# First layer of a two-layer kernel: the first image's front and first projection cut into chunks beside the first steps, and VectorE's work at an image's end one piece later

## The chip, the cores and the metric

The kernel runs on one core of one Trainium2 chip. The metric is the device time of one execution in microseconds; less is better. Before the change the median of five runs is 6506.6 us (6499.82 to 6520.29).

A core has five engines with queues of their own: TensorE (PE, with its weight loads PEld), VectorE (DVE), ScalarE (ACT), GpSimd (POOL) and SyncE (SP, which here only issues transfers). Each engine works through its queue in order; a result that another engine needs is waited for at the head of the queue, with everything behind it.

## What is computed

Two layers over four images of 48 x 48 positions and 128 channels. The first layer, cut to what matters here:

```
xn = groupnorm(x); xin, z = split(xn @ in_proj.T)            # 128 -> 2 x 256
xc = silu(depthwise_conv3x3(xin) + conv_b)                    # 256 channels, 2304 positions
for k in 0..3:          # by rows, by columns, and both backwards
    dts, Bs, Cs = split(x_proj[k] @ xc_k)                     # 8 + 16 + 16 rows
    dt = softplus(dt_proj[k] @ dts + dt_b[k])                 # 256 x 2304
    for n in 0..15:     # states
        h = scan over positions: h = h * exp(dt * A[k, :, n]) + dt * xc_k * Bs[n]
        ys_k += h * Cs[n]
y = sum of the four ys_k (turned back) + D * xc
x = x + out_proj @ (layernorm(y) * silu(z))
```

The second layer (a spectral attention block over 128 x 128 images) isn't touched by the change.

## The kernel before

Channels lie on the 128 partitions, the 256 inner channels as two halves `f`. The 2304 positions are cut into five chunks (`CHUNKS`, line 34): four of 480 and one of 384. An image has four directions in the order 0, 2, 1, 3 (`ORDER`), so there are 16 directions, 80 chunks and, with 16 states each, 1280 *steps*. The main loop (line 508 on) calls `advance` once a step.

**A step** is spread over ten calls of `advance` by `LAGS` (line 470). In one call each engine gets its share of different steps: SP fetches the broadcast rows of B and C (`fetch`), PE spreads a row of B over the partitions into PSUM, tile `pb` (`spread`, lag 3; a single buffer), DVE multiplies it with `du` = dt x xc into `db` (`drive_in`, lag 4; each fourth step POOL does it, from a transferred row), ACT takes the two exponentials `da` (`decay`, lag 4), DVE runs the scan `h` (`scan`, lag 5), POOL multiplies by C into `hc` (`read_out`, lag 5), PE adds the two halves of `hc` into `yp` (`sum_up`, lag 8), and ACT stores `yp` when a chunk is done (`put_away`, lag 9).

**The side work** is written as generators in a list `later`, and `piece()` (line 454) runs one of them up to its next `yield`; `advance` ends with one piece. A generator that has begun keeps its turn until it yields `FREE` or `WAIT`; else the first of the list that needn't wait is taken. The side work is:

- `front(b)` (line 151): load x of image b, its statistics (`bn_stats`), the scaled weights `w`, and for each half f: nine diagonal matrices of the taps `cdiag` and a cleared padded image `pad` on POOL, the input projection `pj` on PE with ACT writing it into `pad`, then nine matmuls per chunk (`pc`) with ACT writing `xc`; a piece holds one input projection or three taps. Silu over all of `xc` comes last.
- `project` (line 217): for each chunk of the next direction px, a transfer of B and C to DRAM (`cd`), two corrections `less`, and the two halves of dt (`pd`); then Softplus over all five chunks. The ring of seven buffers lets it run at most six chunks ahead (`WAIT`).
- `back` (line 271): for each chunk of an image's last direction the layer norm over channels, the gate and the output projection: PE's mean `pm`, DVE subtracts, ACT squares, PE `pv`, ACT's square root, PE's gate `pz` twice, DVE's reciprocal, Silu, POOL multiplies, PE `po`, DVE multiplies, PE `pr`, DVE adds, store.

All matmuls of the side work use one PSUM bank, `pp` (`side`, line 132), so one's result must be taken away before the next one begins.

`Ordered` (line 36) keeps the instructions of PE, DVE, ACT and POOL in the order in which the program calls them, so what stands in front of what on an engine is decided by these calls. The order of SP's transfers is chosen by the framework.

**The order of things.** Line 502: the first image's `front` is run to its end alone, then the first direction's `project` to its end (lines 504, 505), then `drive` computes `du` for the first chunk on POOL, and only then the steps begin. The other images' fronts run beside steps: at the third chunk (m == 2) of an image's first direction the open `back`s are drained and `front(b + 1)` joins `later`. `drive` for the next chunk is called at steps 8 and 12 of a chunk.

Of the kernel before, what the change touches and what calls it, by code (L numbers as in the profile page):

```python
# [10 lines left out]
F32 = mybir.dt.float32  # L11
# [10 lines left out]
L = T * H  # L22
# [31 lines left out]
def layer0(ctx, tc, io, x1_dram):  # L54
# [20 lines left out]


# [14 lines left out]
    on.gpsimd.memset(w_xp, 0.0)  # L91
    for k in range(K):
        src = io["x_proj_wT"][k].rearrange("(f p) c -> p f c", p=128)
        for o, c0, c1 in ((0, R, R + 2 * N), (32, 0, R), (64, R, R + N), (96, R, R + N)):
            nc.sync.dma_start(w_xp[:, k, :, o : o + c1 - c0], src[:, :, c0:c1])
# [35 lines left out]

    def side(name):
        return ps_s.tile([128, 512], F32, tag="pp", name=name)
# [11 lines left out]
    def load_x(b, name):  # L145
        x = one.tile([128, 1, L], F32, tag="x", name=f"{name}{b}")
        for q in range(4):
            nc.sync.dma_start(x[:, 0, q * 576 : (q + 1) * 576], io["xT"][:, b, q * 576 : (q + 1) * 576])
        return x

    def front(b, made):


        x = load_x(b, "x")
        xc = two.tile([128, NF, L], F32, tag="xc", name=f"xc{b}")
        made["xc"] = xc
        yield FREE
# [20 lines left out]
        yield FREE  # L178
        for f in range(NF):
            cdiag = one.tile([128, 9, 128], F32, tag="cdiag", name=f"cdiag{b}_{f}")  # L180
            for j in range(9):
                on.gpsimd.tensor_scalar(cdiag[:, j], ident, cw[:, f, j : j + 1], None, ALU.mult)
            pad = one.tile([128, T + 2, H + 2], F32, tag="pad", name=f"pad{b}_{f}")
            on.gpsimd.memset(pad, 0.0)
            yield FREE
            for s, n in CHUNKS:
                r0, nr = s // H, n // H
                pj = side(f"pj{b}_{f}_{s}")
                on.tensor.matmul(pj[:, 0:n], w[:, f * 128 : (f + 1) * 128], x[:, 0, s : s + n], start=True, stop=True)
                yield  # L190
                on.scalar.activation(
                    pad[:, 1 + r0 : 1 + r0 + nr, 1 : 1 + H],
                    pj[:, 0:n].rearrange("p (r c) -> p r c", c=H),
                    AF.Identity,
                    bias=wb[:, f : f + 1],
                )
            for s, n in CHUNKS:
                r0, nr = s // H, n // H
                pc = side(f"pc{b}_{f}_{s}")
                for j in range(9):  # L200
                    dy, dx = divmod(j, 3)
                    on.tensor.matmul(
                        pc[:, 0:n].rearrange("p (r c) -> p r c", c=H),
                        cdiag[:, j],
                        pad[:, r0 + dy : r0 + dy + nr, dx : dx + H],
                        start=(j == 0),
                        stop=(j == 8),
                    )
                    if j % 3 == 2:
                        yield  # L210
                on.scalar.activation(xc[:, f, s : s + n], pc[:, 0:n], AF.Identity, bias=cb[:, f : f + 1])
            yield FREE
# [3 lines left out]

    def project(b, k, chunks, xc):

        w_dt = two.tile([32 + R, D], F32, tag="w_dt", name=f"w_dt{b}_{k}")
        nc.sync.dma_start(w_dt[32 : 32 + R], io["dt_proj_wT"][k])
        for c in chunks:
            s, n = c.s, c.n
            while done[0] + RING - 1 < c.number:
                yield WAIT
            src = at(xc, k, s, n)
            px = side(f"px{c.t}")
            for f in range(NF):
                on.tensor.matmul(  # L230
                    like(px[0:NX, 0:n], k), w_xp[:, k, f], src[:, f], start=(f == 0), stop=(f == NF - 1)
                )
            yield
            xd = two.tile([32 + R, LC], F32, tag="xd", name=f"xd{c.t}")
            on.scalar.copy(xd[:, 0:n], px[0 : 32 + R, 0:n])
            c.cd = dram.tile([2 * N, LC], F32, tag="cd", name=f"cd{c.t}")
            nc.sync.dma_start(c.cd[:, 0:n], xd[0 : 2 * N, 0:n])

            c.bs = ring.tile([NX, LC], BF16, tag="bs", name=f"bs{c.t}")
            on.scalar.copy(c.bs[:, 0:n], px[0:NX, 0:n])  # L240
            for q in range(2):
                on.tensor.matmul(px[0:NX, 0:n], less[:, q], c.bs[:, 0:n], start=False, stop=True, skip_group_check=True)
                yield
                rows = slice(64 + 32 * q, NX)
                on.scalar.copy(c.bs[rows, 0:n], px[rows, 0:n])
            c.dt = ring.tile([128, NF, LC], F32, tag="dt", name=f"dt{c.t}")
            for f in range(NF):
                pd = side(f"pd{c.t}_{f}")
                on.tensor.matmul(
                    pd[:, 0:n],  # L250
                    w_dt[32 : 32 + R, f * 128 : (f + 1) * 128],
                    xd[32 : 32 + R, 0:n],
                    start=True,
                    stop=True,
                )
                yield
# [249 lines left out]
    for f in range(NF):  # L506
        drive(directions[0][0], f)
# [655 lines left out]
```

## Time and profile before

| what | value |
|---|---|
| median of five runs | 6506.6 us |
| the profiled execution: its time, its span | 6507.24 us, 6505.4 us |
| mean granted clock of TensorE | 0.833 |
| busy in the span: PE, DVE, ACT, POOL | 4834.9, 5268.8, 3052.8, 4727.3 us |
| first scan starts | 224.1 us |
| last scan starts | 4390.4 us |
| last op of the first layer on DVE starts | 4421.11 us |

The steps of the first layer fill 224 to 4390 us; the second layer runs from 4421 us to the end. In the timeline of VectorE the starts of the scans were counted, 80 to a direction. The time from the first scan of a direction to that of the next is, in us:

| image | direction 0 | 2 | 1 | 3 |
|---|---|---|---|---|
| 0 | 276.0 | 256.4 | 240.5 | 276.4 |
| 1 | 281.0 | 257.1 | 240.5 | 280.2 |
| 2 | 280.7 | 256.8 | 244.5 | 278.9 |
| 3 | 246.5 | 240.3 | 240.4 | 270.2 |

Within a direction eight steps that nothing disturbs take 24.1 us with 480 positions and 19.7 with 384. Images 0 to 2 have the next image's front beside directions 0 and 2; image 3 has none.

In the lines that follow, a window's line gives its bounds, its length, then the busy time of PE, PEld, DVE, ACT and POOL with the number of instructions, TensorE's granted clock, the DMA engines' busy share and GB/s. A timeline's line gives start and duration in us, the engine, the program's line (50 for all that go through `Ordered`), the operation, output<-inputs, the shapes and the count; a bracket holds the idle time before it and what ended it. A tile's view lists how long its engine sat idle before the instructions on it, until what, and how many times.

### The profile page before, as it was taken

How to read it: one execution, taken by the hardware profiler on the slowest of the kernel's cores; microseconds unless marked ns; L12 is line 12 of the kernel's file. 1: busy time of each engine (PE TensorE's matmuls, PEld its weight loads, DVE VectorE, ACT ScalarE, POOL GpSimd, SP SyncE). 2: the span in 40 equal slices, each digit the busy share in tenths (PEclk: the TensorE clock that was granted, in tenths of full speed). 3: DMA queues.
4: the chain of work that ended last, by engine and by line, in shares of the span. 5: the costliest groups of instructions: out<-in, count | busy, mean ns of one | idle time of the engine just before them, and what ended most of it. 6: DMA issues, size and time to landing. Idle time of an engine off the chain costs nothing. (4 is left out here: it accounts for less than half of the span.)

```text
span 6505.4 us, 45606 instructions
## 1 busy us (share of the span) xinstructions
PE 4834.9 (74%) x12650; PEld 2229.8 (34%) x12650; DVE 5268.8 (81%) x3784; ACT 3052.8 (47%) x6633; POOL 4727.3 (73%) x2641
## 2 busy tenths in 40 slices
PE   6788778889787888877888777784233498878663
PEld 2244333334333334333333333332122244435332
DVE  0678999887999897899989999983799899963444
ACT  1556666656666665666666656552000133312222
POOL 1588998887998888899888999981665499941222
PEclk9799999999999999999999999997566655556876
DMA  1222322222233232232323322322100100010222
GB/s 26 68 86 90 100 96 96 91 95 85 98 105 96 89 100 87 89 100 95 96 89 104 101 99 99 96 80 58 44 0 1 16 8 4 4 40 8 59 59 58
DMA packets 271777, 457.65 MB, mean 70 GB/s; under 512 B 87134, under 2 KB 196734, under 8 KB 271522
## 3 DMA queue, kind: packets, MB, share of 16 engines
q1 hardware_dynamic: 224546, 438.13, 21.6%
q10 hardware_dynamic: 46976, 16.61, 1.4%
q8 instruction: 99, 1.62, 0.1%
q14 instruction: 156, 1.28, 0.1%
HBM read 419.60 MB, written 35.02 MB: 70 GB/s over the span
## 5 line engine op out<-in xcount | busy, mean ns | idle before, releaser
L50 POOL TENSOR_TENSOR hc<-h,cbc 128x960 f32<-128x960 f32 (+1 forms) x1280 | 2718.1, 2136 | 521.8 <-DVE h L50 363.1
L50 DVE TENSOR_TENSOR_SCAN h<-da,carry,db 128x961 f32<-128x961 f32 (+1 forms) x1280 | 2698.9, 2129 | 94.1 <-ACT carry L50 62.3
L50 PE MATMUL yp<-hc,ident 128*128 128x480 f32 (+1 forms) x5120 | 2292.1, 578 | 0.5 <-POOL hc L50 0.5
L50 ACT ACTIVATE da<-dt,a_neg 128x480 f32<-128x480 f32 (+1 forms) x2560 | 1666.3, 651 | 1300.1 <-DVE h L50 1254.2
L50 PEld LDWEIGHTS yp<-hc,ident 128*128 128x128 f32 x5120 | 1014.7, 200 | 1539.5 <-issue 970.8
L50 DVE TENSOR_TENSOR db<-du,pb 128x960 f32<-128x960 f32 (+1 forms) x960 | 1063.3, 1108 | 411.1 <-PE pb L50 357.2
L50 PE MATMUL pb<-bs,pick 112*128 112x480 bf16 (+1 forms) x960 | 362.8, 378 | 539.9 <-DVE db L50 538.4
L50 POOL TENSOR_TENSOR db<-du,bbc 128x960 f32<-128x960 f32 (+1 forms) x320 | 687.2, 2147 | 0.0
L928 PE MATMUL py<-attn_t,xt 48*128 48x384 f32 x768 | 507.6, 845 | 78.6 <-DVE m L936 71.6
L930 ACT COPY ysb<-py 128x384 f32<-128x384 f32 x384 | 184.3, 480 | 404.0 <-PE py L928 360.8
L928 PEld LDWEIGHTS py<-attn_t,xt 48*128 48x128 f32 x768 | 233.8, 320 | 339.2 <-issue 147.8
L50 PE MATMUL pc<-pad,cdiag 128*128 128x480 f32 (+1 forms) x720 | 301.5, 559 | 7.6 <-ACT xc L50 6.0
L50 POOL TENSOR_TENSOR du<-dt,xc 128x480 f32<-128x480 f32 (+1 forms) x160 | 204.3, 1277 | 120.8 <-ACT dt L50 120.8
L50 ACT COPY db<-carry 128x1 f32<-128x1 f32 x1280 | 228.6, 179 | 35.5 <-DVE db L50 33.0
L50 PE MATMUL px<-xc,w_xp 128*112 128x480 f32 (+1 forms) x320 | 212.1, 793 | 8.8 <-ACT xc L50 4.9
L848 PE MATMUL pat<-ident,s 48*48 48x48 f32 x128 | 13.3, 277 | 275.6 <-POOL s L844 275.6
L50 PE MATMUL yp<-y,ident 128*128 128x480 f32 (+1 forms) x240 | 175.6, 865 | 40.3 <-ACT y L50 40.3
L941 POOL TENSOR_TENSOR zi<-zi,m 128x384 f32<-128x384 f32 x192 | 191.9, 999 | 14.5
L50 PEld LDWEIGHTS <-pick 112*128 112x128 bf16 x960 | 99.3, 103 | 300.1 <-issue 284.6
L939 POOL TENSOR_TENSOR zi<-gw,ysb 128x384 f32<-128x384 f32 x192 | 181.6, 946 | 25.8 <-ACT ysb L930 25.5
L50 PE MATMUL pd<-xd,w_dt 8*128 8x480 f32 (+1 forms) x320 | 176.4, 632 | 25.4 <-ACT bs L50 14.6
L50 ACT COPY carry<-h 128x2 f32<-128x2 f32 x1024 | 194.4, 190 | 0.0
(263 smaller groups left out, 5626.8 us busy)
## 6 DMA issues: line engine op xcount, KB each, us to landing
cbc<-cd SPq DMA_DIRECT2D x512, 480.0 KB
bbc<-cd SPq DMA_DIRECT2D x256, 240.0 KB
cbc<-cd SPq DMA_DIRECT2D x128, 384.0 KB
bbc<-cd SPq DMA_DIRECT2D x64, 192.0 KB
da_wM<-a_wM SPq DMA_DIRECT2D x12, 396.0 KB
x<-in_xT SPq DMA_DIRECT2D x16, 288.0 KB
xr<-in_xT SPq DMA_DIRECT2D x16, 288.0 KB
e_wM<-de_wM SPq DMA_DIRECT2D x12, 384.0 KB
```

The costliest lines, as they stand in the source:

```text
L50: return lambda *args, **kw: self._tc.keep_in_program_order(emit(*args, **kw))
L848: nc.tensor.transpose(pt[:, h], s[:, h], ident[0:T, 0:T])
L928: nc.tensor.matmul(p[:, 0 : HG * T], xt[:, c, j], attn_t[:, b, hs], start=True, stop=True)
L930: nc.scalar.copy(ysb[:, c], py[c])
L939: nc.gpsimd.tensor_mul(zi[:, hs], gr, ysb[:, 1])
L941: nc.gpsimd.tensor_add(zi[:, hs], zi[:, hs], t2)
```

## The change

- The loads of x for the first image come first; `x_proj` is loaded with four transfers into `w_x` and put into place in `w_xp` by four DVE copies, instead of sixteen transfers.
- `front` is split into `open_up` (statistics and scaled weights), `taps`, `project_in` and `convolve`, and `project` gets its inner part as `project_chunk`; for images 1 to 3 they do what they did.
- The first image has a generator of its own, `boot`: both halves' taps and cleared images are made at the very start (the second half's lie in the buffer of the second `xc`), then for each chunk in turn both halves are projected (with one more row of 48 positions as the convolution's halo), convolved, put through Silu, projected for the first direction, and put through Softplus; a chunk is then `ready`.
- The steps begin when the first chunk is ready. During the first direction each step is followed by a second piece, and `boot` stands first in `later`.
- Until the steps begin, `side` goes round four PSUM banks; then it uses `pp` alone as before.
- `drive` is called at steps 11 and 14 of a chunk instead of 8 and 12; in the first direction it first runs pieces until that chunk is ready.
- In `back` there is one more `yield` ahead of each of three DVE operations: the subtraction after pm, the multiplication after po, the addition after pr.

```diff
+    x_first = load_x(0, "x")
...
+    w_x = const.tile([128, K, NF, R + 2 * N], F32, name="w_x")
     for k in range(K):
...
-            nc.sync.dma_start(w_xp[:, k, :, o : o + c1 - c0], src[:, :, c0:c1])
+        nc.sync.dma_start(w_x[:, k], io["x_proj_wT"][k].rearrange("(f p) c -> p f c", p=128))
+    for o, c0, c1 in ((0, R, R + 2 * N), (32, 0, R), (64, R, R + N), (96, R, R + N)):
+        on.vector.tensor_copy(w_xp[:, :, :, o : o + c1 - c0], w_x[:, :, :, c0:c1])
...
+    banks = deque([(ps_s, "pp"), (ps_b, "pb"), (ps_y, "yp0"), (ps_y, "yp1")])
+    begun = [False]
+
     def side(name):
-        return ps_s.tile([128, 512], F32, tag="pp", name=name)
+        pool, tag = banks[0]
+        if not begun[0]:
+            banks.rotate(-1)
+        return pool.tile([128, 512], F32, tag=tag, name=name)
...
+    def boot(chunks, made):
+        pads = [one.tile([128, T + 2, H + 2], F32, tag="pad", name="pad0")]
+        cdiags = [one.tile([128, 9, 128], F32, tag="cdiag", name="cdiag0")]
+        spare = two.tile([128, NF * L], F32, tag="xc", name="spare")
...
+        for f in range(NF):
+            taps(cdiags[f], f)
+            on.gpsimd.memset(pads[f], 0.0)
+        x = x_first
+        yield from open_up(0, x, made)
+        w_dt = load_dt(0, 0)
+        for c in chunks:
+            s0, s1 = (c.s + H if c.s else 0), min(c.s + c.n + H, L)
+            for f in range(NF):
+                for s in range(s0, s1, LC):
+                    yield from project_in(0, f, x, made, pads[f], s, min(LC, s1 - s))
+                yield from convolve(0, f, cdiags[f], pads[f], made["xc"], c.s, c.n)
+            v = made["xc"][:, :, c.s : c.s + c.n]
+            on.scalar.activation(v, v, AF.Silu)
+            yield from project_chunk(c, w_dt, made["xc"])
+            on.scalar.activation(c.dt[:, :, 0 : c.n], c.dt[:, :, 0 : c.n], AF.Softplus)
+            c.ready = True
+            yield FREE
...
@@ back
             on.tensor.matmul(pm[:, 0:n], lnmat, yb[:, f, 0:n], start=(f == 0), stop=(f == NF - 1))
+        yield
         yield
         on.vector.tensor_sub(ys, ys, pm[:, None, 0:n].to_broadcast([128, NF, n]))
...
         yield
+        yield
         on.vector.tensor_mul(xo[:, 0:n], po[:, 0:n], rs[:, 0:n])
...
         yield
+        yield
         on.vector.tensor_add(xo[:, 0:n], xo[:, 0:n], pr[:, 0:n])
...
-    later.append(front(0, images[0]))
-    drain(later[0])
-    nxt = upcoming(0)
-    drain(nxt)
+    first = directions[0]
+    later.append(boot(first, images[0]))
+    while not first[0].ready:
+        piece()
+    begin()
     for f in range(NF):
-        drive(directions[0][0], f)
+        drive(first[0], f)
...
-                if i in (N // 2, N // 2 + 4):
-                    f = int(i > N // 2)
+                if i in (N // 2 + 3, N // 2 + 6):
+                    f = int(i > N // 2 + 3)
                     if m + 1 < len(chunks):
+                        while not (j or chunks[m + 1].ready):
+                            piece()
                         drive(chunks[m + 1], f)
...
                 advance(Step(c, i))
+                if not j:
+                    piece()
```

## The prediction

> **What bounds the kernel now.** I read the span first, then VectorE's timeline with its 1280 scans counted in eights, then the windows, then the single waits.
>
> ```profile
> 0.00:50.00 50.00, 16.74 (x28) 7.24 (x29) 7.07 (x29) 6.55 (x10) 10.37 (x19) 1.00 0.22 42
> 50.00:100.00 50.00, 39.02 (x92) 16.98 (x90) 0.00 (x0) 4.56 (x7) 7.37 (x10) 0.92 0.00 0
> 100.00:150.00 50.00, 43.09 (x95) 18.84 (x94) 0.00 (x0) 6.13 (x9) 0.00 (x0) 0.88 0.07 24
> 150.00:200.00 50.00, 31.90 (x39) 9.20 (x40) 0.00 (x0) 17.54 (x26) 0.00 (x0) 0.57 0.14 45
> 250.00:300.00 50.00, 38.64 (x92) 16.85 (x92) 49.17 (x30) 30.01 (x76) 47.78 (x24) 0.93 0.31 101
> 400.00:450.00 50.00, 49.27 (x133) 23.73 (x132) 38.68 (x24) 24.27 (x61) 36.73 (x18) 1.00 0.22 70
> 500.00:531.00 31.00, 31.00 (x91) 16.32 (x90) 19.55 (x15) 13.99 (x37) 19.91 (x13) 1.00 0.22 63
> ```
>
> Columns: window, length, busy us of PE, PEld, DVE, ACT, POOL, granted clock, DMA share, GB/s. For 200 us DVE does nothing: the first image's front and first projection run alone. At 250 DVE is full (49 of 50); at 400 to 531 PE is full, because the next image's front is woven in one piece per step.
>
> ```profile
> 220.82 1.16 DVE L50 TENSOR_TENSOR db<-du,pb 128x960 f32<-128x960 f32 x1 [195.01 <-PE pb L50]
> 224.14 2.21 DVE L50 TENSOR_TENSOR_SCAN h<-da,carry,db 128x961 f32<-128x961 f32 x1
> ...
> 483.95 0.96 DVE L50 TENSOR_TENSOR db<-du,pb 128x768 f32<-128x768 f32 x1 [1.19 <-PE pb L50]
> ...
> 259.64 0.56 PE L50 MATMUL pb<-bs,pick 112*128 112x480 bf16 x1 [3.27 <-DVE db L50]
> 259.99 3.03 PE L50 MATMUL yp<-hc,ident 128*128 128x480 f32 x4
> 263.02 0.36 PE L50 MATMUL pb<-bs,pick 112*128 112x480 bf16 x1
> ...
> 481.17 2.58 PE L50 MATMUL pc<-pad,cdiag 128*128 128x480 f32 x6
> 483.58 0.33 PE L50 MATMUL pb<-bs,pick 112*128 112x384 bf16 x1
> ```
>
> The first scan is at 224.1. By the count, eight undisturbed steps take 24.1 us (3.01 a step; 2.47 in a chunk of 384). The first direction's 80 scans take 276.0 instead of 232, the second's 256.4 (its first eight 31.0). Where PE is full a step is the sum of its matmuls: one pass of 480 columns is 0.402 us (481.17 to 483.58 is six), so an fp32 matmul is 0.80, a step's own work (two yp, 3/4 of a pb) 1.76, three taps 2.41.
>
> ```profile
>   PE pm L50: 22.8, 11
>   PE po L50: 45.4, 17
>   PE pr L50: 40.9, 20
> ...
> 4398.68 1.16 DVE L50 TENSOR_TENSOR yb<-yb,pm 128x960 f32<-128x960 f32 x1 [6.16 <-PE pm L50]
> 4403.58 3.15 DVE L50 RECIPROCAL ws<-ws 128x480 f32<-128x480 f32 x1 [3.75 <-ACT ws L50]
> 4416.90 0.66 DVE L50 TENSOR_TENSOR ws<-po,ws 128x480 f32<-128x480 f32 x1 [10.16 <-PE po L50]
> 4421.11 0.66 DVE L50 TENSOR_TENSOR ws<-ws,pr 128x480 f32<-128x480 f32 x1 [3.56 <-PE pr L50]
> ```
>
> The tile views: in 20 `back`s DVE waits 109.1 us, 19.9 of it in the bare tail (the 6.16 is mostly the last read-out; 10.16 and 3.56 are `back`'s own). The tail's last `back`, with nothing beside it, takes 4398.68 to 4421.77 = 23.1 us, of which DVE works 5.6.
>
> **Part 1, the start.** Loads: SP now issues x first, and four w_x loads instead of sixteen (10.86 us). 4x0.475 + 0.40 + 0.42 + 0.43 + 4x0.68 + 0.47 puts w_out's issue at 7.1; it lands 1.9 later as now; four new DVE copies (about 1 us, an estimate from the 0.28 of a 128x128) and the old constants put bn_stats at 12.1 to 15.4 instead of 20.98: 5.6 earlier. The taps and clearings of both halves, 2x(5.24+2.18) on POOL, end near 19.5, before `w` is due, so they cost nothing; if ident landed 2 us later they would cost that much. First projection matmul: 28.05 - 5.6 = 22.4.
>
> Chunk 0: input projection, halo and padding 3.1; first half's taps 10.0 (cold rate, as at 45.76); second half 2.0 + 7.8; ACT copy, Silu table and Silu 2.9; projection chain 12.4 as at 165.38, less 0.75 because four banks rotate; Softplus and table 2.2. Together 39.8: ready at 62.2, against 214.6 now.
>
> What then comes ahead of step 0 on PE's in-order queue decides. In the order in which the changed kernel is built, pb of step 0 stands behind chunk 1's first half (18 passes), two input projections and three taps: 0.9 + 10 + 3.2 + 2.7 = 17 us, so pb at 79, first scan near 86: 138 us earlier than 224.1.
>
> Two pieces a step then follow. A boot chunk is 14 pieces, 7 steps. PE's work: 2 input projections 1.6, 18 taps 14.5, px, less and pd 3.6, 7 steps 12.3 = 32.0. Walking its chain, PE waits 1.2 twice for ACT to pad, 2 for xc, Silu and its table, 1.3 + 0.8 for copies of px, and 3.8 while ACT does Softplus, its table, Exp's table and a step's `da` ahead of the padding (1.28+0.88+1.28+1.37): with queueing 44.5 per chunk. From 79, chunk 1's remainder takes 26, chunks 2 and 3 44.5 each, chunk 4 (384 columns, nothing after it) 34.5: 229, at step 27.5.
>
> Then the next direction's projection: 10 steps, 14.4 + 17.6 + 12 of waits = 44. Then image 1's front: 15 steps of six taps at 6.6, 6 of input projections at 4.6, 2.5 of statistics at 3.3, 3 of projection at 4, some 11 of waits for the one bank, less 3 for the short chunk: 155. All in, step 63.5 at 229 + 44 + 155 = 428. The rest, 6x3.01 + 16x2.47 = 57: scan 80 at 485, where it is 500.1 now. Direction 2 starts without a front and should take 240, as image 3's does (240.3), instead of 256.4. **Sum: -15 - 16 = -31 us.** So 107 of the 138 us are given back: TensorE's work did not shrink, and the first 64 steps now cost 5.8 each instead of 3.5 ((447.7 - 224.1)/64).
>
> Bounds: PE's work in that stretch is 75 for boot, 18 for the projection, 80 for the front (90 taps, 10 input projections) and 63.5x1.76 = 112: 285 us. At the 86% that PE reaches over 214 to 531 (273 of 317) the stretch takes 331 instead of my 366, scan 80 is at 450, and part 1 saves 66; at 70% it takes 407 and part 1 loses 10.
>
> A wait of 3.27 us before 259.64 makes the next yp run 3.03 instead of 1.77: each long wait costs 1.3 more; four to eight of them, 5 to 10 us, are in the bounds and not in the sum. The Trainium skill, "TensorE: Matmul & The Clock Gate", section "What's actually happening", says the clock halves after an idle window of about 3.4 us; it speaks against this change, whose waits on Softplus would each be followed by a cold stretch.
>
> ACT: four table loads per boot chunk, 16 more in all, 1.28 each by the trace (2175.59: the next activation starts 0.02 after the load). "ScalarE: Activation LUTs", section "What ACT_TABLE_LOAD costs", adds a drain of about 1.4 us per switch; by it part 1 would lose some 10 us more. The trace shows no such drain.
>
> Queued behind new waits: SP's load of image 1's x waits for boot's last input projection (step 21), with cbc of step 24 behind it, whose buffer is not free before step 24: nothing.
>
> **Part 2, the image's end.** Moving DVE's op one step later removes its own wait, but pb of the following step stands behind po on PE, and DVE's db needs it. Seen at 2193 to 2197: PE waits for POOL's yb, po ends at 2197.0, pb at 2197.4; now DVE waits 1.68 for po, then it would wait about 2.0 for pb. po: 0. pr and pm are short and PE has room: half of their waits outside the tail, (37.3 + 16.6)/2 = -27. Bounds: 0 to -90.
>
> Three more pieces in each `back` have another effect. The pieces of steps 64 to 95 no longer suffice: in the built order the fifth `back` of images 0 and 1 is drained in one go ahead of chunk 2 of the next image, its sub, reciprocal and two last ops back to back on DVE. Now it hides (1.9 of waiting at 1335.8). Bare it costs 23.1 - 5.6 - 1.9 = 15.6 twice: +31 (bounds +16 to +45). **Sum: +4.**
>
> Part 3, du at steps 11 and 14 instead of 8 and 12: the same 1.2 us on POOL, and its first use is four or more steps later: 0. What could hide it no longer: POOL is 95% busy in undisturbed stretches, so a `du` that came late would cost DVE at most its 1.2 per half in the few chunks where POOL lags; it is not seen in the rows, DVE's waits name pb, not du.
>
> **Total -27:** profiled execution 6507.24 (span 6505.4) and median 6506.6 agree to 0.6, so 6480.
>
> **Rivals.** (a) PE stays full in the weave as at 400 to 531: part 1 saves 66, time 6506.6 - 66 + 4 = 6445. For: one piece fills PE to 96% there; against: the pieces of boot need ACT's answer each time. (b) Slower: two pieces a step leave PE half idle and cold. Place: steps 0 to 63; price 63.5 us for each us a step; it decides where the stretch exceeds 366 + 27 = 393 us, 6.2 a step against my 5.8. At 6.5 (413 us) the change is 20 slower, 6527. For: 3.8 us waits and the 3.03 row; against: 250 to 300 shows 0.93 of the clock at 77% busy. (c) DVE's waits for pm, po, pr really vanish (-90, the 109.1 less the tail's 19.9): -31 - 90 + 31 gives 6417. For: po's mean wait outside the tail, 35.2/16 = 2.2 us, is less than a step; against: pb stands behind po on the in-order PE. (d) The overlap does not come about, first scan still near 200: the built order excludes it.
>
> **How the numbers follow.** Forecast 0.43, (a) 0.23, (b) 0.24, (c) 0.10. The forecast's own range is 6455 to 6505. All cases with (b) to 6.7 a step: 6420 to 6540. A measurement tells 0.2% (13 us) from no change: the forecast gives 0.29 faster, 0.12 same, 0.02 slower; (a) and (c) 0.33 faster; (b) 0.03 same, 0.21 slower. Faster 0.62, same 0.15, slower 0.23.
>
> **What would show it.** First scan at 80 to 90; scan 80 near 485 and 80 scans in some 400 us; PE over 70% busy with DVE near 45% to 430; the second direction near 240; two gaps of 15 us or more on DVE at the third chunk of images 1 and 2; po's wait gone and pb's grown. Scan 80 under 455 or over 520 would refute part 1; an image's last direction under 262 (now 276 to 280) part 2.

## The result, and the profile after

The changed kernel takes 6515.02 us (median of 23 runs, 6507.44 to 6527.5), the kernel before 6506.6 (43 runs): a ratio of 1.0014, interval 1.0008 to 1.002. That is some 9 us slower, where 6480 had been forecast. The profiled execution of the changed kernel took 6507.6 us (span 6505.8), which is as fast as the fastest of its 23, that of the kernel before 6507.24 (span 6505.4), close to its median; so most of the 9 us can't be looked for in these two traces. What can be read in them is the first layer, by counting scans.

The windows of the changed kernel that answer to those shown of before (window, length, busy us and instructions of PE, PEld, DVE, ACT, POOL, granted clock, DMA share, GB/s), with the whole stretch from the first chunk's readiness to the end of image 1's front as the last line:

```profile
0.00:50.00 50.00, 23.14 (x56) 12.07 (x56) 9.04 (x33) 7.50 (x12) 18.06 (x29) 1.00 0.19 39
50.00:100.00 50.00, 35.45 (x65) 13.32 (x66) 10.84 (x7) 22.74 (x35) 11.24 (x7) 0.78 0.19 57
100.00:150.00 50.00, 41.17 (x88) 16.98 (x87) 21.31 (x13) 25.61 (x47) 22.13 (x11) 0.85 0.14 48
150.00:200.00 50.00, 38.48 (x90) 16.68 (x89) 24.83 (x15) 28.44 (x55) 20.25 (x10) 0.94 0.13 44
250.00:300.00 50.00, 39.23 (x98) 16.57 (x97) 36.97 (x34) 29.51 (x66) 30.93 (x15) 0.94 0.19 68
400.00:450.00 50.00, 46.97 (x119) 21.43 (x118) 24.05 (x14) 16.25 (x41) 25.27 (x13) 1.00 0.23 69
500.00:531.00 31.00, 29.42 (x83) 13.35 (x82) 29.38 (x22) 22.59 (x57) 27.62 (x17) 1.00 0.34 98
...
62.00:457.00 395.00, 323.71 (x761) 141.87 (x762) 196.41 (x126) 188.50 (x386) 201.59 (x111) 0.92 0.18 57
```

VectorE has work from 84 us on instead of 221. But in the windows shown between 50 and 450 it is busy for a fifth to three quarters of the time, where before it was full in its first windows with steps (49.17 of 50), and TensorE is the busy engine throughout: 323.7 of 395 us. Only at 500 is VectorE full, since image 1's front is out of the way by then.

VectorE's timeline in the stretch with taps (start, duration, operation, idle time before it and what ended it):

```profile
83.61 1.16 DVE L50 TENSOR_TENSOR db<-du,pb 128x960 f32<-128x960 f32 x1 [3.81 <-PE pb L50]
84.68 2.21 DVE L50 TENSOR_TENSOR_SCAN h<-da,carry,db 128x961 f32<-128x961 f32 x1
...
334.08 1.16 DVE L50 TENSOR_TENSOR db<-du,pb 128x960 f32<-128x960 f32 x1 [8.71 <-PE pb L50]
340.73 1.16 DVE L50 TENSOR_TENSOR db<-du,pb 128x960 f32<-128x960 f32 x1 [3.36 <-PE pb L50]
347.37 1.16 DVE L50 TENSOR_TENSOR db<-du,pb 128x960 f32<-128x960 f32 x1 [3.36 <-PE pb L50]
...
505.80 1.81 DVE L50 TENSOR_TENSOR_SCAN h<-da,carry,db 128x769 f32<-128x769 f32 x1
```

The first scan is at 84.68 (before 224.14), and scan 80 at 505.80 (before 500.1). From 334.08 to 340.73 to 347.37 a step takes 6.65 us: with six taps to each step VectorE waits 3.36 us for the spread `pb`, and 8.71 after each fourth step, which has no spread of its own, so that twelve taps lie between two of them.

The starts of the scans, counted as for the kernel before, in us (directions of one image in a row: 0, 2, 1, 3):

| | image 0 | image 1 | image 2 | image 3 |
|---|---|---|---|---|
| before | 276.0 256.4 240.5 276.4 | 281.0 257.1 240.5 280.2 | 280.7 256.8 244.5 278.9 | 246.5 240.3 240.4 270.2 |
| after | 421.1 240.5 241.0 265.5 | 308.9 258.1 241.5 263.2 | 308.9 258.1 241.5 263.4 | 249.3 240.5 240.5 262.0 |

At scan 160, the first of the third direction, the changed kernel is 10.2 us ahead (746.3 against 756.5). Its four directions 3 take 51.6 us less, and its directions 0 of images 1 and 2 take 28 us more each.

Where those 28 us lie, in VectorE's timeline ahead of image 1's third chunk:

```profile
1338.59 1.13 DVE L50 TENSOR_TENSOR yb<-yb,pm 128x960 f32<-128x960 f32 x1
1345.07 3.15 DVE L50 RECIPROCAL ws<-ws 128x480 f32<-128x480 f32 x1 [5.36 <-ACT ws L50]
1358.37 0.66 DVE L50 TENSOR_TENSOR ws<-po,ws 128x480 f32<-128x480 f32 x1 [10.14 <-PE po L50]
1362.59 0.66 DVE L50 TENSOR_TENSOR ws<-ws,pr 128x480 f32<-128x480 f32 x1 [3.56 <-PE pr L50]
1363.16 1.15 DVE L50 TENSOR_TENSOR db<-du,pb 128x960 f32<-128x960 f32 x1
```

This is the fifth `back`, drained with nothing beside it: no scan between 1338.59 and 1363.16, and 19.06 us of waiting (5.36 + 10.14 + 3.56). The tile views (idle time of the engine named ahead of such instructions, times) and the tail:

```profile
  PE pm L50: 8.6, 1
...
  PE po L50: 30.4, 3
...
  PE pr L50: 10.7, 3
```

```profile
4400.29 1.15 DVE L50 TENSOR_TENSOR yb<-yb,pm 128x960 f32<-128x960 f32 x1 [8.55 <-PE pm L50]
4424.36 0.66 DVE L50 TENSOR_TENSOR ws<-ws,pr 128x480 f32<-128x480 f32 x1 [3.56 <-PE pr L50]
```

Before, VectorE waited 11, 17 and 20 times for pm, po and pr. Now it is once, three times and three times: the tail and the two drains. Beside the steps these waits are gone altogether. The first layer ends at 4424.36 where it ended at 4421.11.

### The profile page after: what moved, and what is told of

Same layout as the page of the kernel before. It is cut to its first block, busy times and chain, and to the rows that moved or that the text cites. A ratio compares the mean times of both kernels' runs of the same rounds, so it can differ in the third digit from the quotient of the medians.

```text
span 6505.8 us, 45606 instructions
## 1 busy us (share of the span) xinstructions
PE 4832.8 (74%) x12654; PEld 2225.1 (34%) x12654; DVE 5274.4 (81%) x3788; ACT 3067.3 (47%) x6652; POOL 4729.1 (73%) x2641
## 5 line engine op out<-in xcount | busy, mean ns | idle before, releaser
L50 PE MATMUL pc<-pad,cdiag 128*128 128x480 f32 (+1 forms) x630 | 268.0, 566 | 16.1 <-ACT pad L50 13.1
L1019 POOL TENSOR_TENSOR m<-gw,ysb 128x384 f32<-128x384 f32 x192 | 185.2, 964 | 10.8 <-ACT ysb L1009 10.8
```

The source lines that it names most:

```text
L50: return lambda *args, **kw: self._tc.keep_in_program_order(emit(*args, **kw))
L1019: nc.gpsimd.tensor_mul(t2, gi, ysb[:, 0])
```

## The experiments

The table has what the twelve kernels gave. A ratio is against the kernel before, run on the same chip (its medians there were 6499.7 to 6505.5 us); "scan 160" and "last scan" are starts, "0 + 2" is the time of directions 0 and 2 of images 1 and 2, "3" the sum of the four directions 3, all in us of the profiled execution.

| kernel | median us | ratio, interval | first scan | scan 160 | 0 + 2, images 1, 2 | 3, sum | last scan |
|---|---|---|---|---|---|---|---|
| before | | 1 | 224.1 | 756.5 | 538.1, 537.5 | 1105.7 | 4390.4 |
| after | 6515.0 | 1.0014, 1.0008 to 1.002 | 84.7 | 746.3 | 567.0, 567.0 | 1054.1 | 4389.0 |
| 1 start only | 6496.6 | 0.999, 0.9981 to 0.9999 | 86.4 | 752.4 | 537.1, 537.3 | 1103.5 | 4379.1 |
| 2 yields only | 6513.2 | 1.0017, 1.0008 to 1.0026 | 222.6 | 754.7 | 564.6, 565.1 | 1051.7 | 4389.9 |
| 3 one piece after boot | 6481.8 | 0.996, 0.9946 to 0.9973 | 85.1 | 713.5 | 567.1, 567.0 | 1052.8 | 4355.4 |
| 4 no drain | 6487.2 | 0.9975, 0.9965 to 0.9984 | 84.8 | 749.1 | 551.3, 554.6 | 1053.5 | 4361.1 |
| 5 du as before | 6512.1 | 1.0014, 1.0006 to 1.0023 | 85.4 | 754.4 | 563.7, 563.7 | 1057.3 | 4390.3 |
| 6 = 3 and 4 | 6443.7 | 0.9914, 0.99 to 0.9927 | 85.4 | 713.8 | 551.5, 554.6 | 1052.7 | 4325.6 |
| 7 po's yield only | 6474.7 | 0.9954, 0.9941 to 0.9968 | 222.1 | 753.4 | 541.2, 540.9 | 1064.9 | 4352.0 |
| 8 pm's and pr's only | 6496.9 | 0.9986, 0.9977 to 0.9995 | 222.2 | 754.5 | 552.3, 552.3 | 1065.9 | 4373.8 |
| 9 pieces split | 6507.2 | 1.0005, 0.9996 to 1.0014 | 85.5 | 743.7 | 568.3, 568.4 | 1050.2 | 4383.3 |
| 10 = 6, two taps | 6406.4 | 0.985, 0.9836 to 0.9863 | 84.4 | 696.5 | 535.9, 536.7 | 1052.7 | 4279.5 |
| 11 = 10, split | 6399.3 | 0.9836, 0.9822 to 0.9849 | 85.6 | 691.1 | 535.9, 536.7 | 1052.8 | 4274.1 |
| 12 = 11, po's yield only | 6433.9 | 0.99, 0.9884 to 0.9917 | 85.7 | 691.2 | 544.2, 543.7 | 1069.8 | 4307.7 |

### The change taken apart

Kernel 1 is the changed kernel with the three `yield`s and du's steps put back:

```diff
         yield
-        yield
         on.vector.tensor_sub(ys, ys, pm[:, None, 0:n].to_broadcast([128, NF, n]))
...
         yield
-        yield
         on.vector.tensor_mul(xo[:, 0:n], po[:, 0:n], rs[:, 0:n])
...
         yield
-        yield
         on.vector.tensor_add(xo[:, 0:n], xo[:, 0:n], pr[:, 0:n])
...
-                if i in (N // 2 + 3, N // 2 + 6):
-                    f = int(i > N // 2 + 3)
+                if i in (N // 2, N // 2 + 4):
+                    f = int(i > N // 2)
```

> The changed kernel with back's three yields and du's steps (8 and 12) put back: the start alone. Theory (start and image's end are separate, and the start is worth what the scans of the changed kernel show up to scan 160, 756.5 - 746.3): 10 us faster than the kernel before, 4 to 16; first scan near 85, directions 0 and 2 of image 0 near 421 and 241, direction 3 of images 0 to 2 back at 276 to 280, direction 0 of images 1 and 2 back at 281. Rival A (the whole loss of 9 us sits in the start, and the image's end is even): 9 us slower than before. Rival B (du's later steps are what shortened direction 3): direction 3 is back at 276 to 280 as well, so e1 does not tell B from the theory; the next kernel does.

Kernel 2 is the kernel before with these three `yield`s alone, as the change has them.

> The kernel before with back's three yields alone (du at 8 and 12, the old start). Theory (the yields shorten direction 3 by 8 to 17 us an image, 52 in all, and lay the fifth back bare ahead of chunk 2 of images 1 and 2, 28 each, and lengthen the tail by 3): 8 to 20 us slower than before; direction 3 near 263 to 266, direction 0 of images 1 and 2 near 309. Rival B (du's later steps shortened direction 3): direction 3 stays at 276 to 280 and the kernel is some 55 to 60 us slower. Rival C (the 28 us of direction 0 come from the front and the du steps, not from the drained back): direction 0 of images 1 and 2 stays near 281 and the kernel is some 40 to 50 us faster.

The start alone makes the kernel 0.1% faster (0.9981 to 0.9999), some 6 us. The yields alone make it 0.17% slower, with direction 3 at 261 to 266 and direction 0 of images 1 and 2 at 307 to 308, as the theory had it; so rival B (du) and rival C fall. Both halves of the change do what they do by themselves, in different places.

Kernel 5 is the changed kernel with du back at steps 8 and 12 (the second edit of kernel 1 alone).

> The changed kernel with du's steps put back from 11 and 14 to 8 and 12. Theory (du's move is worth nothing, as forecast: 1.2 us on POOL per half, four steps or more ahead of its use): within 5 us of the changed kernel, last scan 4384 to 4394, no direction different by more than 5 us. Rival (the start alone at 0.9990 and the yields alone at 1.0017 add to 1.0007 and not to the 1.0014 of the changed kernel, so the late du costs the rest): 5 us faster than the changed kernel, spread over direction 0 and 2 of every image.

Its ratio is that of the changed kernel, 1.0014, and its last scan 1.3 us later: du's move is worth nothing that can be measured. It is not without effect: directions 0 and 2 together take 3.3 us less in images 1 and 2 with du as before, and scan 160 comes 8.1 us later. The two cancel.

### What the start gives back

Kernel 3 runs the second piece of a step only while `boot` is unfinished:

```diff
-    later.append(boot(first, images[0]))
+    boot_gen = boot(first, images[0])
+    later.append(boot_gen)
...
-                if not j:
+                if boot_gen in later:
                     piece()
```

> The changed kernel, but the second piece of a step is run only while boot is unfinished, so that the next direction's projection and image 1's front go one piece a step as in images 1 and 2. Theory (six taps and two round trips through ACT in one step are what makes the stretch 29 us too long; one piece hides nearly all of it behind DVE): steps after boot cost about 3.5 us instead of 5, scan 80 near 415 to 440, direction 2 near 256 to 275; together 30 to 60 us faster than the changed kernel, 6455 to 6485. Rival (TensorE's work and its waits in all decide, however they are spread): scan 160 stays near 746, time within 10 us of 6515.

Scan 80 is at 443.5, 3.5 us past the expected bounds, direction 2 takes 270.0 instead of 240.5, and scan 160 is 32.8 us earlier than in the changed kernel (by the ratios 0.0054, 35 us). TensorE's work is the same; it is spread over 30 us more of direction 2. One window of it, to set beside the changed kernel's 250 to 300 above:

```profile
250.00:300.00 50.00, 46.72 (x117) 19.46 (x116) 49.17 (x30) 37.27 (x90) 46.69 (x24) 0.97 0.32 103
```

VectorE is full (49.17) and TensorE busier as well (46.72 against 39.23): with one piece a step, the projection of direction 2 hides behind VectorE; with two, VectorE has 36.97. So the second piece, after `boot` has ended, costs what VectorE could have done meanwhile. And with one piece of three taps, VectorE's wait in a step is short, from the same trace:

```profile
413.40 0.95 DVE L50 TENSOR_TENSOR db<-du,pb 128x768 f32<-128x768 f32 x1 [1.19 <-PE pb L50]
417.28 0.96 DVE L50 TENSOR_TENSOR db<-du,pb 128x768 f32<-128x768 f32 x1 [1.19 <-PE pb L50]
```

Kernel 9 leaves two pieces in each step of the first direction, but lays one of them between the spread and `sum_up`:

```diff
         for lag, stage in LAGS:
+            if stage is sum_up and window[0] is not None and window[0].c.number < len(CHUNKS):
+                piece()
...
-                if not j:
-                    piece()
```

> The changed kernel with the first direction's second piece moved: it runs ahead of sum_up and not behind the first one, so that two matmuls of yp or a spread lie between any two pieces on TensorE while ACT answers. TensorE's work is the same. Theory (the projection of direction 2 takes 58 us and not 44, and the boot chunks 48 and 45, because the second of two pieces in a row waits for ACT to empty the one bank): the waits of 0.6 to 1.5 us ahead of less, pd and pj go, boot's last pd at 215 to 225 instead of 232, scan 80 at 480 to 490 instead of 506, 12 to 25 us faster than the changed kernel. Rival (the stretch is long because six taps and a step's own work come between two spreads, whatever their order): scan 80 at 500 to 510, within 6 us of the changed kernel.

The theory was that the second of two pieces in a row waits for ACT to empty the one bank. Scan 80 is at 502.4, only 3.4 us earlier, and the time 0.0009 lower (some 6 us, with intervals that overlap). That is the rival's: ACT's answers are a small part. (The 58 us set against 44 there hold the fifth chunk, which the forecast had in the sum for image 1's front.) The taps run at the same pace as in the changed kernel:

```profile
334.14 1.16 DVE L50 TENSOR_TENSOR db<-du,pb 128x960 f32<-128x960 f32 x1 [8.49 <-PE pb L50]
340.79 1.16 DVE L50 TENSOR_TENSOR db<-du,pb 128x960 f32<-128x960 f32 x1 [3.36 <-PE pb L50]
```

The step is 6.65 us again in both places tried: what counts in these steps is how much of TensorE's work stands between two spreads.

### What the image's end gives back

Kernel 4 is the changed kernel without the draining of the backs ahead of chunk 2; the next front then simply stands behind them in the list:

```diff
-                while backs:
-                    drain(backs.popleft())
                 coming = front(b + 1, images[b + 1])
```

> The changed kernel without the loop that drains the open backs ahead of chunk 2: image b+1's front simply stands behind them in the list. Theory (the two bare backs cost 28 us each): direction 0 of images 1 and 2 near 281 to 288, 40 to 56 us faster than the changed kernel, 6459 to 6475, and faster than before. Rival (the extra 28 us are the fifth back's work on TensorE, ACT and POOL, which only moves to the steps behind it, or push the front into direction 2): direction 0 loses at most 10 or direction 2 grows by what it loses, 0 to 15 us faster than the changed kernel.

Direction 0 of images 1 and 2 falls from 308.9 to 283.6 and 285.3, about the 25 us of the bare stretch; but direction 2 grows from 258.1 to 267.7 and 269.3, since the front begins later. Net 12 to 16 us an image: 0.0039 in the ratio, 25 us where the theory had 40 to 56, and a kernel 0.25% faster than the kernel before (0.9965 to 0.9984). The theory named the place rightly and the rival the part that only moves. The fifth `back` in its trace:

```profile
1341.53 1.13 DVE L50 TENSOR_TENSOR yb<-yb,pm 128x960 f32<-128x960 f32 x1
...
1352.55 3.13 DVE L50 RECIPROCAL ws<-ws 128x480 f32<-128x480 f32 x1
...
1369.69 0.63 DVE L50 TENSOR_TENSOR ws<-po,ws 128x480 f32<-128x480 f32 x1
...
1377.44 0.63 DVE L50 TENSOR_TENSOR ws<-ws,pr 128x480 f32<-128x480 f32 x1
```

None of the four has a bracket: scans run between them, and nothing is waited for.

Kernels 7 and 8 are the kernel before with po's yield alone, and with pm's and pr's alone:

```diff
@@ kernel 7
         yield
+        yield
         on.vector.tensor_mul(xo[:, 0:n], po[:, 0:n], rs[:, 0:n])
@@ kernel 8
         yield
+        yield
         on.vector.tensor_sub(ys, ys, pm[:, None, 0:n].to_broadcast([128, NF, n]))
...
         yield
+        yield
         on.vector.tensor_add(xo[:, 0:n], xo[:, 0:n], pr[:, 0:n])
```

> The kernel before with back's yield ahead of the multiplication after po alone. The forecast on record (po gains nothing: the spread of the next step's row stands behind po on TensorE, and VectorE would wait for that instead): direction 3 stays at 276 to 280. Theory now (po's mean wait of 2.2 us is covered by VectorE's 3 us step, and the spread is there in time): direction 3 shorter by 4 to 9 us an image; and five pieces more in five backs, so that only po and pr of the fifth back are drained bare, direction 0 of images 1 and 2 longer by 5 to 14.

> The kernel before with back's yields ahead of the subtraction after pm and the addition after pr, without the one after po. The forecast on record (half of the waits outside the tail): direction 3 shorter by 27/4 = 7 us an image. Theory now (all of the 37.3 + 16.6 us outside the tail): 10 to 14 us an image. In direction 0 of images 1 and 2 ten pieces more are left to the drain: 12 to 25 us longer.

Kernel 7 is 0.46% faster than the kernel before. Its directions 3 take 40.8 us less (1064.9 against 1105.7), 4.5 to 13.9 an image, and direction 0 of images 1 and 2 is only 3.1 and 3.4 us longer: the expected 5 to 14 for the drain was too much, five more pieces still nearly fit. Kernel 8 takes 39.8 us off the directions 3, as the theory then had it, and loses 14 in each of the two directions 0. The three together take off 52 to 54, not 81: they partly remove the same idle time.

What VectorE waited for in direction 3 of image 1, the lines on PE, in the kernel before and then in kernel 7 (which operation, on what, us in total, times, longest):

```profile
DVE ws L50 <- PE po L50: 8.9, 4, 2.9
DVE ws L50 <- PE pr L50: 8.0, 4, 2.4
DVE db L50 <- PE pb L50: 4.2, 3, 2.2
...
DVE yb L50 <- PE pm L50: 3.8, 2, 2.8
```

```profile
DVE db L50 <- PE pb L50: 5.1, 6, 2.3
DVE ws L50 <- PE pr L50: 3.7, 4, 1.4
DVE yb L50 <- PE pm L50: 1.1, 1, 1.1
```

The 8.9 us for po are gone, and the wait for the spread, which was forecast to take their place, grew by 0.9. Image 1 is the most favourable of the three: read in the same way over directions 3 of images 0 to 2, the wait for the spread grew from 7.9 to 15.3 us, while 26.6 for po went. With kernel 8's yields it grew to 32.7, with all three in the changed kernel to 29.9, where 62.3 for pm, po and pr went. So what the forecast named does happen; it takes back a part of the gain, 22 of 62 us with all three yields. The waits for pr and pm, which kernel 7 does not touch, fell to 3.7 and 1.1 in image 1. One of the four places, TensorE and VectorE in kernel 7:

```profile
2181.95 4.32 DVE L50 TENSOR_TENSOR_SCAN h<-da,carry,db 128x961 f32<-128x961 f32 x2
2181.97 1.88 PE L50 MATMUL po<-yb,w_out 128*128 128x480 f32 x4 [1.30 <-POOL yb L50]
...
2186.19 0.63 DVE L50 TENSOR_TENSOR ws<-po,ws 128x480 f32<-128x480 f32 x1
```

Here po ends at 2183.85 while VectorE is in two scans until 2186.2, and nothing is waited for. The extra yield does more than move VectorE's operation one step down: the pieces behind it, pr and the backs that follow, shift against the steps as well.

### Together

Kernel 6 has the edits of kernels 3 and 4.

> The changed kernel with both edits: the second piece only while boot is unfinished, and no draining of the backs ahead of chunk 2. Theory (the two losses lie in different places, image 0 and images 1 and 2, and add): 6502 x (0.9960 + 0.9975 - 1.0014) = 6456, 50 to 58 us under the changed kernel; scan 160 near 713, direction 0 plus direction 2 of images 1 and 2 near 552 each. Rival (pieces put off in one place crowd the next: image 1's front ends later and pushes the projection of direction 1 or 3 into a bare drain): direction 1 or 3 of image 0 grows by 10 us or more, 6465 to 6480.

6443.7 us, 12 under the 6456 of the sum (by the ratios 0.0006, inside the intervals): the two add, and scan 160 (713.8) and the pairs of directions are those of kernels 3 and 4. No direction 1 or 3 grew.

Kernel 10 is kernel 6 with finer pieces in the fronts of images 1 to 3:

```diff
-    def convolve(b, f, cdiag, pad, xc, s, n):
+    def convolve(b, f, cdiag, pad, xc, s, n, stops=(2, 5, 8)):
...
-            if j % 3 == 2:
+            if j in stops:
                 yield
...
@@ front
-                yield from convolve(b, f, cdiag, pad, xc, s, n)
+                yield from convolve(b, f, cdiag, pad, xc, s, n, (1, 3, 5, 8))
```

> The kernel with one piece after boot and no draining (6444 us), with the fronts of images 1 to 3 cut finer: pieces of 2, 2, 2 and 3 taps instead of 3, 3 and 3. Theory (a step with three taps is 4.2 us of TensorE against VectorE's 3.0, one with two 3.4, so a step with taps loses 0.4 instead of 1.2 and the steps with no spread make up for part of it): of the some 36 us a front costs, 10 to 15 are saved, three times: 20 to 45 us faster than 6444. Rival (ten more pieces a front push the last projection into a bare drain at the end of direction 2, or the sum of TensorE's work over the stretch decides): direction 2 no shorter or longer, 6440 to 6460.

Kernel 11 is kernel 10 with the second piece, while `boot` is unfinished, laid ahead of `sum_up` as in kernel 9.

> The kernel with two-tap pieces, and the second piece of a step, which is run only while boot is unfinished, laid ahead of sum_up. Theory (ACT's answer is waited for by the second of two pieces in a row): boot ends some 8 to 15 us earlier and the kernel is as much faster than the one with two-tap pieces. Rival (boot's chunks wait for ACT's Softplus, tables and Exp, which stand ahead of the padding however the pieces lie): within 5 us of it.

Two taps bring 17 us at scan 160 and 16 and 18 us in images 1 and 2; by the ratios, 0.0064 or 42 us, where 20 to 45 had been expected. In the trace of kernel 11, the same stretch as shown of kernel 3 (a chunk of 384 with pieces of 3, 2 and 2 taps of 480 columns):

```profile
417.21 0.96 DVE L50 TENSOR_TENSOR db<-du,pb 128x768 f32<-128x768 f32 x1 [1.19 <-PE pb L50]
420.28 0.96 DVE L50 TENSOR_TENSOR db<-du,pb 128x768 f32<-128x768 f32 x1 [0.38 <-PE pb L50]
426.25 0.96 DVE L50 TENSOR_TENSOR db<-du,pb 128x768 f32<-128x768 f32 x1 [1.57 <-PE pb L50]
```

After a piece with three taps VectorE waits 1.19, after one with two 0.38, and 1.57 for two such steps where the POOL step lies between. In kernel 11 boot's last pd starts at 231.05, in kernel 10 at 234.89: 3.8 us, and 5.4 at scan 160, where the theory had 8 to 15; by the ratios 0.0014, with intervals that overlap. That is nearer the rival.

Kernel 12 is kernel 11 with po's yield alone.

> The kernel with two-tap pieces and the second piece ahead of sum_up (6399 us), with back's yields ahead of the subtraction after pm and the addition after pr taken out, so that the one after po alone is left. Theory (po's yield alone brought 41 us of the 52 in direction 3; the other two bring the rest, and with no drain they cost no more than places in the list): direction 3 longer by 2 to 5 us in each image, directions 0 and 2 of images 1 to 3 within 3 us, 6 to 16 us slower than 6399. Rival (ten pieces fewer in each image's backs let the next front begin ten steps earlier, and the first 32 steps of direction 0 lose nothing): direction 0 shorter by 5 us or more, within 5 us of 6399 or faster.

It is 0.0064 slower than kernel 11, some 42 us, where 6 to 16 had been expected. The directions 3 take 17 us more; but directions 0 and 2 of images 1 and 2 take 8.3 and 7.0 us more as well. Eights of steps differ there both ways; the one from the 64th takes 36.3 and 35.4 instead of 27.6. Neither theory nor rival had that. Its trace shows VectorE waiting 7.66 us for ACT there (at 1459.59), which takes the Softplus of five chunks with a table load on either side just before (1451.23 to 1458.23). Kernel 11 has no such wait in that place; why the two come to differ stays open. Kernel 11 is the best of all: 1.64% faster than the kernel before.

## Why the prediction was wrong, by its own steps

**The start: right.** First scan forecast at 86, measured 84.7; chunk 0's dt at 62.2, measured 62.9; boot's end 229, measured 231.8 to 232.7. The first chunk's input projection was expected at 22.4 and came at 26.67; the rest of chunk 0's chain was some 3.6 us shorter than the 39.8 forecast (whose terms, as written, add to 39.65). So this end is right by two errors of about 4 us that cancel.

**The stretch: the failed step.** The 366 us from 62 to 428 were 395, to 457 (the last taps of image 1). In the forecast's own terms:

- boot: 167 us forecast (62 to 229), 172 measured, up to the first px of the next projection at 234.
- "Then the next direction's projection: 10 steps, 14.4 + 17.6 + 12 of waits = 44". Ten steps are twenty pieces, and a chunk has five, so this is four of five chunks. They took 48 (234 to 282).
- "Then image 1's front: ... 155", 20 us too little. It holds the fifth chunk as "3 of projection at 4" (12 us; 11 measured, 372 to 383, since the ring had no place for it before and the front's first half keeps its turn) and the taps as 15 steps at 6.6, less 3 for the short chunk (96; 51 and 49 measured, 321 to 372 and 408 to 457). The term that failed is the rest: 6 steps of input projections at 4.6, 2.5 of statistics at 3.3 and some 11 of waits for the one bank, 47 us in 8.5 steps. It took 39 (282 to 321) and 25 (383 to 408), 64 us, in which 11 scans started.

The forecast put down waits for the one bank alone there. The two longest waits of VectorE in these 64 us have other causes:

```profile
301.50 5.24 POOL L50 TENSOR_SCALAR cdiag<-ident,cw 128x128 f32<-128x128 f32 x9
306.69 2.17 POOL L50 MEMSET pad<- 128x2500 f32 x1
314.34 1.16 DVE L50 TENSOR_TENSOR db<-du,pb 128x960 f32<-128x960 f32 x1 [7.92 <-PE pb L50]
...
382.96 1.28 ACT L50 ACT_TABLE_LOAD   x1
384.25 4.42 ACT L50 ACTIVATE dt<-dt 128x768 f32<-128x768 f32 x5
392.46 2.22 DVE L50 TENSOR_TENSOR_SCAN h<-da,carry,db 128x961 f32<-128x961 f32 x1 [8.25 <-ACT carry L50]
```

At the first half's start POOL makes the nine tap matrices and clears the padded image until 308.86; ACT's padding starts at 308.89, TensorE's second input projection at 309.61 after 4.78 us idle, and the next spread and VectorE stand behind these. At the second half's start ACT takes the Softplus of the projection's five chunks, then a second table load up to 390.87, and only then a step's exponentials. Together the two waits are 16 us. That they make up most of the 17 is read from these rows; it is not separated from the 2.5 steps more that ran there, and no kernel was run without them.

What follows the stretch took 49 us in place of 57, since more steps had been done inside it. So scan 80 came 21 us late, at 505.8 and not at 485, and a saving of 31 became 10.

TensorE's own work was put at 285 us for this stretch and it was busy for 323.7. At the granted 0.92, 323.7 would be 298 (an estimate from that one line), so some 26 of these 39 us are passes below the full rate. By the same estimate, window by window, about half of them lie in boot's chunks (13 us from the four clocks below), which had been costed from rows of the same kind and ended on time, and most of the rest in image 1's front (0.92 and 0.93 in its two parts); the 5 to 10 us that the forecast kept outside its sum were too few.

Rival (b) gave 393 us as the point from which the change stops paying, and 395 is what came, with a first layer that ends 3.3 us later. That it fits so well is partly luck: the steps behind the stretch took 8 us less than forecast and the rest of the layer 9 more. Its mechanism did not hold: TensorE was not half idle but 82% busy (323.7 of 395). The page of the Trainium skill "TensorE: Matmul & The Clock Gate", section "What's actually happening", was set against the change for the waits on Softplus. The trace agrees in part. TensorE's rows behind a padding that waits for Softplus (three taps, six passes, take 2.58 in such a row at the full rate, as at 481.17 before, and 2.20 with 384 columns, as at 449.39):

```profile
105.15 4.41 PE L50 MATMUL pc<-pad,cdiag 128*128 128x480 f32 x6 [3.79 <-ACT pad L50]
153.08 4.34 PE L50 MATMUL pc<-pad,cdiag 128*128 128x480 f32 x6 [2.37 <-ACT pad L50]
197.66 3.75 PE L50 MATMUL pc<-pad,cdiag 128*128 128x384 f32 x6 [3.91 <-ACT pad L50]
```

After each of the three waits the next piece runs at little over half its rate, 1.6 to 1.8 us lost each time, some 5 in all; ahead of the first, TensorE was slow already (two passes at 99.39 took 1.97). The granted clock was 0.77 in the first of boot's chunks beside steps (62 to 106 us), 0.89 in the second, 0.96 and 0.97 behind. So the rule bears on 5 us of the 29 by these lines, and not on the whole.

What the forecast did not ask is whether two pieces a step were needed after `boot`. Kernel 3 shows that they cost 33 us, and the lines of the changed kernel and of kernels 3 and 11 show why: VectorE's wait in a step with six taps is 3.36, with three 1.2, and with two 0.4 (the last two in a chunk of 384).

**Direction 2 of image 0: right,** 240 forecast and 240.5 measured.

**The image's end: a sum near the truth from wrong terms.** +4 was forecast. From scan 160 to the end of the first layer kernel 2 takes 6.4 us more than the kernel before (4425.7 - 754.7 against 4421.1 - 756.5), most of it in the tail, and the changed kernel, with du's later steps, 13.5 more (4424.4 - 746.3). But:

- "po: 0" was wrong. Kernel 7 takes 40.8 us off the directions 3 by po's yield alone. That the spread stands behind po on TensorE was true, and VectorE's waits for it did grow, by 7 us over three images; that they would be as long as the 26.6 us for po was read from one place (2193 to 2197), where TensorE had become slow.
- pm and pr: -27 forecast, -39.8 measured (kernel 8). All three: -52.
- The two bare drains: +31 forecast; direction 0 of images 1 and 2 takes 53 us more in kernel 2 and 56 in the changed kernel. The drain itself was sized nearly right, at 15.6: in the changed kernel the bare stretch is 24.6 us, 19.06 of it idle (the longest gap 10.14, where one of 15 or more had been named as the sign), and the two eights of steps where the fifth `back` lay before are 7.2 shorter (48.2 against 55.4), 17 net. Two things were left out. The first eight steps of direction 0 take 29.9 instead of 24.1: the fourth `back`'s operations behind po and pr fall there (1270.21 and 1276.91), where in the kernel before they were in direction 3 (1256.78 and 1263.10), so part of what direction 3 gains is only moved. And the eight from the 64th takes 31.0 instead of 25.8 (26.1 in kernel 2, where du is not moved). Rival (c), that the waits vanish, was right on the waits (11, 17 and 20 of them down to 1, 3 and 3) and had left out this moved work and the waits for the spread.

**du: 0 forecast, nothing measured** (kernel 5), as the sum of two effects of 7 and 8 us: dearer by 3.3 in each of images 1 and 2, cheaper in image 0.

**Total.** -27 forecast; in the traces the first layer ends 3.3 us later. Of the 30 between, 21 are the start up to scan 160, some 5 the steps from scan 160 to the last, and 5 the tail: from last scan to last operation it takes 35.3 us instead of 30.7, as pieces are left over for it.

Open: the measured 9 us against 3.3 in the traces. The part after the first layer took 2081 to 2098 us in the fourteen profiled executions, and its code is the same in all, so one execution of each does not settle it.

## What to carry to other kernels

In this kernel, work that was moved beside the loop did not become free; it cost what the loop's own bottleneck engine could not do meanwhile. Put as little of it between two of the loop's instructions as fits in the other engine's slack, and let it go on for longer: two pieces in place of one cost 33 us here, and three taps in place of two 42. Where side work has a point at which it must be finished, count its pieces against the steps before adding one: three more in each back gave 52 us in one direction and cost 56 in the next, at and around a drain that the order did not need; without the drain 25 came back.

## What had not been expected of the hardware

TensorE is not equally fast in the two kernels at the image's end, though its work is the same. The windows round a po of the kernel before, and round one of kernel 7:

```profile
2186.00:2199.00 13.00, 8.86 (x16) 3.45 (x15) 11.22 (x9) 7.39 (x17) 12.15 (x6) 0.74 0.23 79
```

```profile
2174.00:2187.00 13.00, 8.98 (x23) 4.02 (x23) 12.79 (x10) 8.39 (x19) 11.69 (x6) 1.00 0.18 64
```

TensorE ran 16 matmul instructions in the one and 23 in the other, in nearly the same busy time (8.86 and 8.98 us), at a granted clock of 0.74 and 1.00. From the kernel before, inside its window:

```profile
2189.92 0.36 PE L50 MATMUL pb<-bs,pick 112*128 112x480 bf16 x1 [3.30 <-DVE db L50]
...
2193.45 3.57 PE L50 MATMUL po<-yb,w_out 128*128 128x480 f32 x4 [0.84 <-POOL yb L50]
```

TensorE had stood idle for 3.30 us ahead of the spread, and four passes of po took 3.57 us; in kernel 7 the idle time there was at most 2.21, and po took 1.88. The Trainium skill ("TensorE: Matmul & The Clock Gate", section "What's actually happening") puts the change of state at an idle window of about 3.4 us; here passes were slow behind 3.30 us, and behind 2.37 in the row at 153.08 above. Over the whole direction 3 of image 1 the granted clock rose from 0.92 to 0.97.

One reading is a loop: a wait of VectorE leaves TensorE without work, that slows it, and that lengthens VectorE's next wait. It would explain why waits that kernel 7 doesn't touch became shorter with po's. It is not shown: the 3.30 us above ended with a `db` that VectorE made behind two scans, without having waited, and kernel 7 also moves the pieces behind po against the steps.
